# A convolution and whitening kernel: three x buffers instead of four, earlier read-back, one spin product a wait, and part of the packing on ScalarE

## The chip, the cores and the metric

The kernel runs on one core of a Trainium2 chip. The metric is the time of one execution in device microseconds; lower is better. Before the change, three runs gave 902.16, 902.56 and 902.67 us, so the median is 902.56 us. The engines are called as in the profile: PE (TensorE), DVE (VectorE), ACT (ScalarE), POOL (GpSimd) and SP (SyncE, which here only issues DMAs).

## The reference, cut to what matters

```python
# x: (4, 64, 256, 256) float32; L = 256, 64 channels, 4 images
def conv(x):                      # layer 0
    hx, hy = implicit_filter(...), implicit_filter(...)      # two small MLPs with sin, times a decay
    k = einsum('ijk,imk->ijmk', hx, hy)                      # per channel: an outer product of two 256-tap filters
    y = irfft2(rfft2(x, 512) * rfft2(k, 512))[..., :L, :L]   # a causal 2-D convolution, per channel
    return y + x * bias

def whiten(x):                    # layer 1
    x1 = x.transpose(1, 0, 2, 3).reshape(64, -1)
    x1_s = x1[:, ::9]                                        # every ninth pixel
    mean1 = x1_s.mean(-1)
    cov = x1_s @ x1_s.T / n + 0.01 * I
    W = isqrt_newton_schulz(cov, 5)                          # 64 x 64
    return (W @ (x1 - mean1)).reshape(...)
```

The filter of each channel is an outer product, so the 2-D convolution is two 1-D convolutions, and each of these is a product with a 256 x 256 Toeplitz matrix. No output pixel can be made before the covariance of all four images is known, because `W` depends on all of them.

## The kernel before, in words

**Two halves.** The first half makes the convolved images and writes them to a DRAM buffer `y_d`. The second half reads them back, multiplies by `W` and writes the output. Between them stands a short chain of small products, `whitening` (L460), that makes `W`.

**The first half.** A step is one channel group of 8 channels (`g`, 0 to 7) of one image (`n`, 0 to 3), so there are 32 steps, listed in `steps` (L107, L108). Groups 0 to 5 run one after the other, each over the four images; then the last two groups run image by image, so that image 0 is whole after step 25, and the others after steps 27, 29 and 31. A step has four chunks of two channels (`c` = 0, 2, 4, 6), and the text below calls chunk `c` of step `i` simply (i, c). For each chunk `group` (L394) issues the first Toeplitz products of this chunk together with the second Toeplitz products of the chunk two places earlier, 80 products in all. ACT then copies the first result out of PSUM (L409, four copies) and DVE adds bias times x to the second result and leaves it in the x tile (L412, two instructions). The eight PSUM banks hold two such groups. The very first and last chunks go through `half_group` (L266).

**What SP issues after each group.** SP's queue is in order. After each group come: `store` (L420), two DMAs of 256 KB from the x tile to `y_d` (L425); `load_x` (L100, issued at L588) of one chunk, 512 KB, of the step two ahead, into one of four x tiles; a block of the Toeplitz matrices of a later channel group, if the table `blocks` (L370 to L376) names this place; and, if the table `early` (L378) names it, the read-back of one piece of `y_d`, 2 MB, by `load_next` (L357).

**Packing.** For the covariance every ninth pixel has to be gathered from the x tile into the tile `samp[n]`. `pack_ops` (L313) makes nine instructions, one for each offset `s` (`copy_predicated` on DVE, L319). For groups 6 and 7 it is called for four channels at a time, for the others for eight. The instructions wait in a list `todo`, and after each group `pack(2.92)` (L385) hands out about 2.92 us of them by a cost that each carries. `covariance(n)` (L327) is 58 products over `samp[n]`; for image n - 1 it is put before chunk 2 of group 7 of image n. The last four channels of the last step are packed on PE (`pack_by_pe`).

**Read-back and homes.** A piece is 1/8 of an image, a tile of 128 x 4096 floats. It is read into a tile that the first half no longer needs. `homes` (L347) lists 13 such tiles in order: `e` (two tiles of `epool`), `t` (three Toeplitz tiles), `s` (four `samp` tiles) and `i` (four x tiles). Nine pieces are read by `early`, the other four behind the last step; 19 more follow as outputs leave.

**The chain.** `whitening` alternates one or two 64 x 64 products on PE with a small operation on DVE or ACT. In each wait `spin` (L437) puts products of the identity that nobody reads on PE: `spin(2)` six times in the loop of the chain (L522, L532, L540).

**The second half.** For each piece four rounds of products with `W` (L635); ACT adds the mean's share to one result (L639) and DVE to the other (L640), both writing back into the piece, and a DMA writes it out (L645). The piece's columns are held as two halves of 2048, and round `w` makes columns `w * 512` to `w * 512 + 511` of each half. Piece 0 leaves in four DMAs (two runs of 2 KB per partition each), piece 1 and the last two in two DMAs (two runs of 4 KB), all others in one (16 KB per partition). SP issues the DMAs of piece 0 and of the last 13 pieces, POOL the rest.

Of the kernel before, what the change touches and what calls it, by code (L numbers as in the profile page):

```python
# [38 lines left out]
F32 = mybir.dt.float32  # L39
I32 = mybir.dt.int32  # L40
AF = mybir.ActivationFunctionType
ALU = mybir.AluOpType
# [3 lines left out]
NB, C, L = 4, 64, 256  # L46
P, H2 = 128, 2
EMB, ORDER = 33, 64
PIX = L * L
CG = 8  # L50
HP = P // 2
STEP = 9
# [2 lines left out]
EPS = 0.01  # L55
N_ITER = 5
GW = P + L
FP = 4096

TURN = 6.283185  # L60
# [4 lines left out]
def conv_whiten_kernel(ctx: ExitStack, tc: tile.TileContext, a: dict, out: bass.AP):  # L65
    nc = tc.nc
    x = a["x"]

    const = ctx.enter_context(tc.tile_pool(name="const", bufs=1))
    xpool = ctx.enter_context(tc.tile_pool(name="xpool", bufs=4))  # L70
    epool = ctx.enter_context(tc.tile_pool(name="epool", bufs=2))
    spool = ctx.enter_context(tc.tile_pool(name="spool", bufs=NB))
    tpool = ctx.enter_context(tc.tile_pool(name="tpool", bufs=3))
    o1pool = ctx.enter_context(tc.tile_pool(name="o1pool", bufs=4))
# [25 lines left out]
    def load_x(t, g, n, c):  # L100
        nc.sync.dma_start(
            out=t[:, c : c + 2],
            in_=x[n, g][:, c : c + 2],
        )


    steps = [(g, n) for g in range(C // CG - 2) for n in range(NB)]  # L107
    steps += [(g, n) for n in range(NB) for g in range(C // CG - 2, C // CG)]  # L108

    x_tiles = [xpool.tile([P, CG, H2, L], F32, tag="in", name=f"x{u}") for u in range(4)]  # L110
    for c in range(0, CG, 2):
        load_x(x_tiles[0], *steps[0], c)
# [15 lines left out]


    rows = const.tile([P, STEP], F32, tag="rows", name="rows")  # L130
    pick = const.tile([P, STEP, P], F32, tag="pick", name="pick")

    def load_pick(lo, hi):
# [44 lines left out]
    nc.scalar.dma_start(out=g0_d[CG:], in_=taps[ORDER : ORDER + CG])  # L178
    nc.gpsimd.dma_start(out=g_d, in_=taps)
    nc.gpsimd.tensor_copy(rows, mask[:, NB - 1, 0, :])  # L180
    busy(22)

    def new_toeplitz(g):
# [129 lines left out]
    def pack_ops(g, n, yt, cs):  # L313
        def op(s):
            nj = (L - s + STEP - 1) // STEP
            src = yt[:, cs, :, s : s + STEP * (nj - 1) + 1 : STEP].rearrange("p c b j -> p b j c")
            dst = samp[n][:, :, 0:nj, g * CG + cs.start : g * CG + cs.stop]
            m = mask[:, n, :, s : s + 1].unsqueeze(3).to_broadcast([P, H2, nj, cs.stop - cs.start])
            nc.vector.copy_predicated(dst, m, src)  # L319

        cost = 0.3 + 1.5e-3 * H2 * NJ * (cs.stop - cs.start)
        return [(cost, lambda s=s: op(s)) for s in range(STEP)]

    cov = const.tile([P, C + 1], F32, tag="cov", name="cov")
    nc.gpsimd.memset(cov, 0.0)
# [1 line left out]
    def covariance(n):  # L327
# [18 lines left out]

    homes = [  # L347
        {"t": (tpool, "toep"), "s": (spool, "samp"), "i": (xpool, "in"), "e": (epool, "extra")}[k]
        for k in "eetssiistitis"
    ]  # L350

    def load_y(i):
# [16 lines left out]


    blocks = {}
    for g in range(1, C // CG):
        first = 16 * g - 14 if g < C // CG - 1 else 16 * g - 22
        for part in range(8):
            k = first + (part * 12 // 8 if g < C // CG - 2 else part)
            blocks[k // 4, k % 4 * 2] = (g, part)  # L376

    early = {  # L378
        (26, 4): 1, (27, 0): 1, (27, 4): 1, (28, 0): 1, (29, 2): 1, (30, 0): 1, (31, 0): 1, (31, 2): 1, (31, 4): 1
    }  # L380
    orders = [list(range(L // HP)), list(reversed(range(L // HP)))]

# [77 lines left out]
    def whitening(i15, ones):  # L460
# [57 lines left out]
        for k in range(1, N_ITER - 1):  # L518
            pq = product(T, T, f"pq{k}")
            if before is not None:  # L520
                next_z(k - 1, before)
            spin(2)  # L522
            Q = Qs[k % 2]
            nc.vector.tensor_copy(Q, pq)
# [25 lines left out]
        W = place(C)  # L550
# [6 lines left out]
    with tc.manual_schedule(  # L557
# [61 lines left out]
    for i, (n, q) in enumerate(pieces):  # L619
        yt = loaded.pop(i)  # L620

        v = yt.rearrange("p (v f) -> p v f", v=2)
        o = out[n, q].rearrange("p (v f) -> p v f", v=2)

        part = 512 if i == 0 else 1024 if i == 1 or i > len(pieces) - 3 else 2048
        for w in range(FP // 1024):


            cols = slice(w * 512, (w + 1) * 512)
            po = [  # L630
                psA.tile([P, 512], F32, tag="psA", name=f"po_{n}_{q}_{w}_{u}") for u in range(2)
            ]
            for k in range(2):
                for u in range(2):
                    nc.tensor.matmul(  # L635
                        po[u][halves[k]], lhsT=W[halves[u]], rhs=v[halves[u], k, cols],
                        start=True, stop=True,
                    )
            nc.scalar.activation(v[:, 0, cols], po[0], AF.Identity, bias=shift)  # L639
            nc.vector.tensor_scalar(v[:, 1, cols], po[1], shift, None, ALU.add)  # L640
            end = (w + 1) * 512
# [64 lines left out]
```

## Time and profile before

| what | value |
|---|---|
| median of three runs | 902.56 us |
| profiled execution, first to last instruction (its span) | 902.1 us, 0.4 us below the median |
| PE busy | 781.2 us, 87% |
| DVE busy | 581.5 us, 64% |
| ACT busy | 395.5 us, 44% |
| DMA | 285.61 MB |
| first product of the convolution | 16.49 us |
| last product of the convolution | 619.4 us |
| first product with `W` | 643.25 us |
| first output DMA issued | 645.57 us |
| last product with `W` done | about 847 us |

The shares are means over stages with different limits. Until 619 us PE is busy all the time; from 646 us on it is the DMA engines that are (PE is busy 82 of the 140 us from 700 to 840 us); between lie 24 us of packing, covariance and chain. A share of the whole span says little here: each part of the change has to be held against its own stage.

### The profile page before, as it was taken

The numbers are of one execution on the slowest core, as the hardware profiler recorded it, in microseconds if no ns is written. First come the engines' busy times: TensorE is split into PE (matmuls) and PEld (weight loads), VectorE is DVE, ScalarE is ACT, GpSimd is POOL, SyncE is SP. The second block draws the span as 40 slices with busy tenths as digits, with TensorE's granted clock in tenths as the row PEclk, the third lists the DMA queues.
The fourth block names the chain that finished last, engine by engine and source line by source line (L and its number), as shares of the span: only waits on it lengthen the run. The fifth ranks groups of instructions, "written<-read, shape, count | busy, mean of one in ns | idle before, by whom it ended". The sixth has DMA issues, their size and how long they took to land.

```text
span 902.1 us, 28046 instructions
## 1 busy us (share of the span) xinstructions
PE 781.2 (87%) x11928; PEld 647.5 (72%) x11928; DVE 581.5 (64%) x801; ACT 395.5 (44%) x676; POOL 14.5 (2%) x40
## 2 busy tenths in 40 slices
PE   8999999999999999999999999999999565666200
PEld 7999999999999999999999999999533111212000
DVE  3487778877888778877888877877688332233200
ACT  2655554545455555545454444442487232233200
POOL 1000000000000000000000000000010000000000
PEclk9999999999999999999999999999999766866755
DMA  7988889798788888888997899979999999999998
GB/s 209 327 262 252 242 261 271 234 273 251 247 263 261 244 264 259 258 250 267 293 275 241 285 351 356 335 237 390 375 401 429 430 432 432 429 434 430 430 430 355
DMA packets 117912, 285.61 MB, mean 317 GB/s; under 512 B 8891, under 2 KB 91116, under 8 KB 110108
## 3 DMA queue, kind: packets, MB, share of 16 engines
q1 hardware_dynamic: 113436, 244.94, 79.0%
q0 software_dynamic: 3056, 37.95, 10.0%
q8 instruction: 95, 1.56, 0.7%
q10 hardware_dynamic: 1296, 0.93, 0.4%
q14 instruction: 29, 0.24, 0.1%
HBM read 149.35 MB, written 134.44 MB: 315 GB/s over the span
## 4 chain that ended last, share of the span: by engine, by line
PE 74%; DMA 11%; another core or an unknown queue 7%; DVE 0%; issue 0%; SPq 0%; ACT 0%; POOLq 0%; DVEq 0%
PE p L220 64%; DMA out_dram<-yi 5%; DMA yi<-y_d 5%; PE po L635 4%; PE pc L333 2%; PE ph L252 1%; PE pk L300 1%; PE spin L442 1%; DMA toep<-g_d 0%; PE busy L152 0%; PE pm L158 0%; SPq L357 0%; DMA scratch<-in_zw_dram 0%; DVE yi L640 0%
## 5 line engine op out<-in xcount | busy, mean ns | idle before, releaser
L220 PE MATMUL p<-toep,x 64*64 64x64 f32 (+3 forms) x5040 | 579.5, 284 | 0.8 <-issue 0.8
L220 PE MATMUL p<-toep,o 64*64 64x64 f32 (+3 forms) x5040 | 579.5, 284 | 0.0
L220 PEld LDWEIGHTS p<-toep,x 64*128 64x128 f32 (+1 forms) x5040 | 535.7, 166 | 24.4 <-issue 1.3
L220 PEld LDWEIGHTS p<-toep,o 64*128 64x128 f32 (+1 forms) x5040 | 536.7, 166 | 10.7 <-issue 0.2
L409 ACT COPY o<-p 64x512 f32<-64x512 f32 x504 | 292.8, 581 | 294.2 <-PE p L220 286.6
L319 DVE COPY_PREDICATED samp<-mask,x 128x464 f32<-128x464 int32 (+3 forms) x351 | 297.2, 847 | 9.8 <-DVE x L412 0.2
L412 DVE SCALAR_TENSOR_TENSOR x<-x,bias,p 128x512 f32<-128x512 f32 x252 | 179.8, 744 | 121.3 <-PE p L220 117.3
L635 PE MATMUL po<-yi,chain 64*64 64x512 f32 x1024 | 143.7, 720 | 60.4 <-DMA yi<-y_d 60.4
L640 DVE TENSOR_SCALAR yi<-po,shift 128x512 f32<-128x512 f32 x128 | 96.1, 751 | 109.0 <-PE po L635 100.7
L635 PEld LDWEIGHTS po<-yi,chain 64*64 64x64 f32 x1024 | 48.0, 162 | 155.2 <-issue 150.5
L639 ACT ACTIVATE yi<-po,shift 128x512 f32<-128x512 f32 x128 | 88.0, 687 | 116.7 <-PE po L635 116.0
L333 PE MATMUL pc<-samp 128*64 128x65 f32 x464 | 14.9, 223 | 0.0
L333 PEld LDWEIGHTS pc<-samp 128*64 128x64 f32 x464 | 14.3, 137 | 0.3
L645 POOL DMA_DIRECT2D out_dram<-yi x19 | 10.5, 554 | 130.5 <-DMA out_dram<-yi 55.1
L606 POOL TENSOR_SCALAR chain<-ident 64x64 f32<-64x64 f32 x2 | 1.0, 519 | 606.6 <-PE ph L252 606.6
L286 DVE COPY o<-ph 64x256 f32<-64x256 f32 x8 | 3.4, 422 | 9.7 <-PE ph L252 9.6
L152 PE MATMUL busy<-idle 128*128 128x128 f32 x64 | 9.4, 307 | 0.0
L152 PEld LDWEIGHTS busy<-idle 128*128 128x128 f32 x64 | 8.9, 222 | 0.2 <-issue 0.2
L300 PE MATMUL pk<-x,pick 128*128 128x56 f32 (+1 forms) x72 | 8.3, 292 | 0.0
L300 PEld LDWEIGHTS pk<-x,pick 128*128 128x128 f32 x72 | 8.1, 192 | 0.1
L442 PE MATMUL spin<-ident 128*128 128x128 f32 x50 | 7.9, 292 | 0.0
L286 ACT COPY o<-ph 64x256 f32<-64x256 f32 x8 | 2.9, 368 | 10.7 <-DMA toep<-g_d 9.2
(93 smaller groups left out, 77.4 us busy)
## 6 DMA issues: line engine op xcount, KB each, us to landing
x<-in_x_dram SPq DMA_DIRECT2D x128, 512.0 KB, 5.3
y_d<-x SPq DMA_DIRECT2D x256, 256.0 KB, 3.5
yi<-y_d SPq DMA_DIRECT2D x32, 2048.0 KB, 15.6
out_dram<-yi POOLq DMA_DIRECT2D x17, 2048.0 KB, 67.7
out_dram<-yi SPq DMA_DIRECT2D x11, 2048.0 KB, 32.9
toep<-g_d SPq DMA_DIRECT2D x28, 256.0 KB, 6.3
toep<-g_d SPq DMA_DIRECT2D x29, 192.0 KB, 5.7
out_dram<-yi SPq DMA_DIRECT2D x4, 1024.0 KB, 32.8
```

The costliest lines, as they stand in the source:

```text
L152: nc.tensor.matmul(p, lhsT=idle[:, 0:P], rhs=idle[:, P : 2 * P], start=True, stop=True)
L220: mm = nc.tensor.matmul(ps[q : q + w, m, HP * k : L], lhsT=src[parts, k // 2, m * P + q : m * P + q + w], rhs=t[parts, : stop : -1] if k e ...
L300: nc.tensor.matmul(pk[:, b, :, 0:nj], lhsT=pick[:, (s - b) % STEP, :], rhs=yt[:, cs, b, s : s + STEP * (nj - 1) + 1 : STEP], start=(s == 0 ...
L319: nc.vector.copy_predicated(dst, m, src)
L333: nc.tensor.matmul(pc[half], lhsT=samp[n][:, b, j, 0:C], rhs=samp[n][:, b, j, :], start=(b == 0 and j < 2), stop=(b == H2 - 1 and j >= NJ ...
L409: nc.scalar.copy(o1[to], units[u][0][0][fr])
L412: nc.vector.scalar_tensor_tensor(x2[:, c2 + u], x2[:, c2 + u], bias[:, ch : ch + 1], units[u][1][0], ALU.mult, ALU.add,)
L442: nc.tensor.matmul(p, lhsT=ident, rhs=ident, start=True, stop=True)
L635: nc.tensor.matmul(po[u][halves[k]], lhsT=W[halves[u]], rhs=v[halves[u], k, cols], start=True, stop=True,)
L639: nc.scalar.activation(v[:, 0, cols], po[0], AF.Identity, bias=shift)
L640: nc.vector.tensor_scalar(v[:, 1, cols], po[1], shift, None, ALU.add)
L645: issue.dma_start(out=o[:, :, end - part : end], in_=v[:, :, end - part : end])
```

## The change

1. The x tiles are three instead of four, and `load_x` fetches the next step instead of the one after it. `x_of(i)` gives a step's tile. `epool` gets the tile that is freed, so there are still 13 homes, in the order `eeessstititis`.
2. `LATE = 3`: the last three channel groups instead of two run image by image, so images are whole after steps 22, 25, 28 and 31.
3. `blocks` is a table with new places and another order of the parts; `early` names (23, 4), (23, 6), (24, 0), (24, 4) and (27, 2) for one piece each, and (30, 2) and (31, 2) for two each. That is nine pieces, as before.
4. Of the packing of four channels, the instruction with `s == 0` becomes two ACT instructions (one for each `b`) that multiply by a new constant `base` (0 or 1) and so write all pixels; the other eight stay on DVE and write over it. `base` is made on POOL.
5. `spin(1)` instead of `spin(2)` at the three places in the loop of the chain.
6. A piece's columns are ordered so that round `w` makes 1024 adjacent ones; the output's layout and the host's transposition follow. The bytes per DMA stay, in one run per partition instead of two.

```diff
+LATE = 3
...
-    xpool = ctx.enter_context(tc.tile_pool(name="xpool", bufs=4))
-    epool = ctx.enter_context(tc.tile_pool(name="epool", bufs=2))
+    xpool = ctx.enter_context(tc.tile_pool(name="xpool", bufs=3))
+    epool = ctx.enter_context(tc.tile_pool(name="epool", bufs=3))
...
-    steps = [(g, n) for g in range(C // CG - 2) for n in range(NB)]
-    steps += [(g, n) for n in range(NB) for g in range(C // CG - 2, C // CG)]
+    steps = [(g, n) for g in range(C // CG - LATE) for n in range(NB)]
+    steps += [(g, n) for n in range(NB) for g in range(C // CG - LATE, C // CG)]
...
+    def x_of(i):
+        return x_tiles[(i + 1) % 3]
...
+    nc.gpsimd.tensor_copy(base, mask[:, :, :, 0])
...
-            nc.vector.copy_predicated(dst, m, src)
+            if s or cs.stop - cs.start == CG:
+                nc.vector.copy_predicated(dst, m, src)
+                return
+            for b in range(H2):
+                nc.scalar.activation(dst[:, b], src[:, b], AF.Copy, scale=base[:, n, b : b + 1])
 
         cost = 0.3 + 1.5e-3 * H2 * NJ * (cs.stop - cs.start)
-        return [(cost, lambda s=s: op(s)) for s in range(STEP)]
+        return [(cost if s or cs.stop - cs.start == CG else 0.0, lambda s=s: op(s)) for s in range(STEP)]
...
-        for k in "eetssiistitis"
+        for k in "eeessstititis"
...
-    for g in range(1, C // CG):
-        first = 16 * g - 14 if g < C // CG - 1 else 16 * g - 22
-        for part in range(8):
-            k = first + (part * 12 // 8 if g < C // CG - 2 else part)
-            blocks[k // 4, k % 4 * 2] = (g, part)
+    for g, (first, groups) in {
+        1: (2, 12), 2: (18, 12), 3: (34, 12), 4: (46, 12), 5: (57, 12), 6: (69, 12), 7: (82, 5)
+    }.items():
+        for at, part in enumerate((0, 2, 1, 3, 4, 6, 5, 7)):
+            k = first + at * groups // 8
+            blocks.setdefault((k // 4, k % 4 * 2), []).append((g, part))
 
     early = {
-        (26, 4): 1, (27, 0): 1, (27, 4): 1, (28, 0): 1, (29, 2): 1, (30, 0): 1, (31, 0): 1, (31, 2): 1, (31, 4): 1
+        (23, 4): 1, (23, 6): 1, (24, 0): 1, (24, 4): 1, (27, 2): 1, (30, 2): 2, (31, 2): 2
     }
...
-            spin(2)
+            spin(1)
             Q = Qs[k % 2]
...
-                spin(2)
+                spin(1)
                 T, M = Ts[k % 2], Ms[k % 2]
...
-                spin(2)
+                spin(1)
 
                 T = place(2 * C, rows=C)
...
-            load_x(x_tiles[1], *steps[1], c)
+            load_x(x_of(1), *steps[1], c)
         for i, (g, n) in enumerate(steps):
-            xt = x_tiles[i % 4]
+            xt = x_of(i)
...
-                if g == C // CG - 1 and n > 0 and c == 2:
+                if g == C // CG - 2 and n > 0 and c == 2:
                     covariance(n - 1)
...
-                if i + 2 < len(steps):
-                    load_x(x_tiles[(i + 2) % 4], *steps[i + 2], c)
-                if (i, c) in blocks:
-                    tg, part = blocks[i, c]
+                if 0 < i < len(steps) - 1:
+                    load_x(x_of(i + 1), *steps[i + 1], c)
+                for tg, part in blocks.get((i, c), ()):
...
-        v = yt.rearrange("p (v f) -> p v f", v=2)
-        o = out[n, q].rearrange("p (v f) -> p v f", v=2)
-
-        part = 512 if i == 0 else 1024 if i == 1 or i > len(pieces) - 3 else 2048
+        v = yt.rearrange("p (w v f) -> p w v f", v=2, f=512)
+
+        part = 1024 if i == 0 else 2048 if i == 1 or i > len(pieces) - 3 else 4096
...
-                issue.dma_start(out=o[:, :, end - part : end], in_=v[:, :, end - part : end])
+                issue.dma_start(out=out[n, q][:, end - part : end], in_=yt[:, end - part : end])
```

More of the change, by code (lines that the diff above doesn't have):

```diff
@@ L104, in load_x @@
         )
-    steps = [(g, n) for g in range(C // CG - 2) for n in range(NB)]
-    steps += [(g, n) for n in range(NB) for g in range(C // CG - 2, C // CG)]
-    x_tiles = [xpool.tile([P, CG, H2, L], F32, tag="in", name=f"x{u}") for u in range(4)]
+    steps = [(g, n) for g in range(C // CG - LATE) for n in range(NB)]
+    steps += [(g, n) for n in range(NB) for g in range(C // CG - LATE, C // CG)]
+    x_tiles = [xpool.tile([P, CG, H2, L], F32, tag="in", name=f"x{u}") for u in range(3)]
+    def x_of(i):
+        return x_tiles[(i + 1) % 3]
     for c in range(0, CG, 2):
-        load_x(x_tiles[0], *steps[0], c)
+        load_x(x_of(0), *steps[0], c)
         if c == 0:
@@ L130, in conv_whiten_kernel @@
     rows = const.tile([P, STEP], F32, tag="rows", name="rows")
+    base = const.tile([P, NB, H2], F32, tag="base", name="base")
     pick = const.tile([P, STEP, P], F32, tag="pick", name="pick")
@@ L620, in conv_whiten_kernel @@
         yt = loaded.pop(i)
-        v = yt.rearrange("p (v f) -> p v f", v=2)
-        o = out[n, q].rearrange("p (v f) -> p v f", v=2)
-        part = 512 if i == 0 else 1024 if i == 1 or i > len(pieces) - 3 else 2048
+        v = yt.rearrange("p (w v f) -> p w v f", v=2, f=512)
+        part = 1024 if i == 0 else 2048 if i == 1 or i > len(pieces) - 3 else 4096
         for w in range(FP // 1024):
-            cols = slice(w * 512, (w + 1) * 512)
             po = [
@@ L635, in conv_whiten_kernel @@
                     nc.tensor.matmul(
-                        po[u][halves[k]], lhsT=W[halves[u]], rhs=v[halves[u], k, cols],
+                        po[u][halves[k]], lhsT=W[halves[u]], rhs=v[halves[u], w, k],
                         start=True, stop=True,
                     )
-            nc.scalar.activation(v[:, 0, cols], po[0], AF.Identity, bias=shift)
-            nc.vector.tensor_scalar(v[:, 1, cols], po[1], shift, None, ALU.add)
-            end = (w + 1) * 512
+            nc.scalar.activation(v[:, w, 0], po[0], AF.Identity, bias=shift)
+            nc.vector.tensor_scalar(v[:, w, 1], po[1], shift, None, ALU.add)
+            end = (w + 1) * 1024
             if end % part == 0:
                 issue = nc.sync if i == 0 or i + len(homes) >= len(pieces) else nc.gpsimd
-                issue.dma_start(out=o[:, :, end - part : end], in_=v[:, :, end - part : end])
+                issue.dma_start(out=out[n, q][:, end - part : end], in_=yt[:, end - part : end])
         if i + len(homes) < len(pieces):
@@ L702 @@
     r = run_bass_kernel_spmd(nc, [arrays], core_ids=[0])
-    y = np.asarray(r.results[0]["out_0_dram"]).reshape(NB, PIX // H2 // FP, H2, C, H2, FP // 2)
-    return np.ascontiguousarray(y.transpose(0, 3, 4, 1, 2, 5)).reshape(NB, C, L, L)
+    y = np.asarray(r.results[0]["out_0_dram"]).reshape(NB, PIX // H2 // FP, H2, C, FP // 1024, H2, 512)
+    return np.ascontiguousarray(y.transpose(0, 3, 5, 1, 4, 2, 6)).reshape(NB, C, L, L)
```

## The prediction

> **What bounds the kernel now.** The page's busy table and slices come first, then the chain that ended last, stage by stage.
>
> ```profile
> PE 781.2 (87%) x11928; PEld 647.5 (72%) x11928; DVE 581.5 (64%) x801; ACT 395.5 (44%) x676; POOL 14.5 (2%) x40
> DMA  7988889798788888888997899979999999999998
> L220 PE MATMUL p<-toep,x 64*64 64x64 f32 (+3 forms) x5040 | 579.5, 284 | 0.8 <-issue 0.8
> ```
>
> The last row carries the first half: 126 groups take 579.5 us, so 4.6 us each, and PE idled 0.8 us before all of them. Nothing in the first half can make PE faster; an edit there can only make it wait. The chain then shows what lies between the halves:
>
> ```profile
> 636.41 0.29 PE pq L457 x2
> 636.71 0.64 PE spin L442 x4
> 637.35 0.26 PE pm L457 x2
> ...
> 643.25 27.70 PE po L635 x256
> ```
>
> PE goes from product to spin to product without a hole, so the unread products are on the path. The third stage is read from stretches of time (PE, PEld, DVE, ACT, POOL, clock, DMA share, GB/s):
>
> ```profile
> 508.00:520.00 12.00, 12.00 (x268) 11.34 (x268) 9.49 (x16) 4.66 (x8) 0.00 (x0) 1.00 1.01 358
> 534.00:546.00 12.00, 12.00 (x216) 11.29 (x217) 9.94 (x17) 4.96 (x9) 0.00 (x0) 1.00 1.03 393
> 570.00:580.00 10.00, 10.00 (x172) 9.46 (x170) 8.88 (x15) 5.37 (x10) 0.00 (x0) 1.00 1.00 380
> 646.00:662.00 16.00, 16.00 (x152) 5.66 (x148) 13.99 (x19) 12.88 (x19) 2.51 (x4) 1.00 0.97 345
> 664.00:700.00 36.00, 35.67 (x336) 12.55 (x329) 30.89 (x43) 28.33 (x42) 3.74 (x7) 1.00 1.01 431
> ```
>
> From 664 us the DMA engines are full at 431 GB/s. After the first output there are 32 pieces to write and 19 to read, 51 x 2.10 MB = 107 MB, or 248 us at that rate; the span has 256 us left. So the end is the moment `W` is known plus a fixed amount of traffic. The first three rows are stretches of the first half in which single pieces are read back: there, too, the DMA share is 1.0, at only 358 to 393 GB/s. These rows decide the prediction.
>
> **Part 1, the spins (faster).** Three turns of the loop, two waits each: six places lose one product of two passes, half of a spin's 0.64 us, so 0.32 us at most. PE then stands until its operand is there. In the timeline the first place reads:
>
> ```profile
> 636.64 0.71 PE L442 MATMUL spin<-ident 128*128 128x128 f32 x4
> 636.75 0.22 DVE L524 COPY chain<-pq 64x64 f32<-64x64 f32 x1 [0.31 <-PE pq L457]
> ...
> 637.28 0.33 PE L457 MATMUL pm<-chain 64*64 64x64 f32 x2
> ```
>
> One product ends at 636.96. The copy ends at 636.97, and PE starts 0.05 us (cov at L341 to pd) to 0.14 us (L503 to pq) after such an end, so `pm` starts at 637.02 to 637.11 instead of 637.28: 0.17 to 0.26 us. The same sum at the other five gives 0.24 to 0.32, 0.29 to 0.32, 0.17 to 0.26, 0.30 to 0.32 and 0.15 to 0.24. Together 1.3 to 1.7 us, I take 1.5. It reaches the end only if the DMA queue is empty by then. Before, the loads run out at about 645 us, when the rate drops to 201 GB/s for two microseconds; afterwards one piece fewer is asked for in the last two steps, so the queue is empty sooner. The clock is 1.00 through the chain, and PE would stand at most 0.15 us at a time. The Trainium skill (TensorE: Matmul & The Clock Gate, "Why this matters for your kernels") warns of PE gaps over about 3 us; no gap here comes near, so this rule would add nothing.
>
> **Part 2, one run per partition in the output DMAs (faster).** Only piece 0, piece 1 and the last two change; the others were contiguous. Stretches: 382 GB/s while piece 0 leaves in 2 KB runs (648 to 652 us), 412 in 4 KB runs (654 to 656), 431 in 16 KB runs, 416 at the end (890 to 898). Piece 0: 2.10 MB at 412 instead of 382 saves 0.4 us; piece 1 between 412 and 431, 0.2; the last two, 4.2 MB between 416 and 431, 0.2. Sum 0.8 us. Bounds: 0, and 3.8 if the whole shortfall of 646 to 662 us (16 x (1 - 345/431) = 3.2) and of the end (0.6) went; most of that is start-up, so I stay near the bottom.
>
> **Part 3, the first copy of four channels (nothing).** 15 packs of four channels give up one DVE instruction each:
>
> ```profile
> L319 DVE COPY_PREDICATED samp<-mask,x 128x232 f32<-128x232 int32 x60 | 37.6, 627 | 1.5
> L135 ACT ACTIVATE pick<-ident,rows 128x128 f32<-128x128 f32 x9 | 3.0, 394 | 0.1
> L309 ACT COPY samp<-pk 128x58 f32<-128x58 f32 x2 | 0.5, 226 | 12.1 <-DVE samp L319 10.8 <-PE pk L300 1.3
> ```
>
> DVE loses 15 x 0.63 = 9.4 us. ACT gains 30 instructions of 116 elements, between the rows of 58 (0.23) and 128 (0.39), so 0.36 each, 11 us; it waits 286.6 us for PE in this stage. There is a new wait: DVE's other eight write over what ACT wrote. Behind ACT's four copies (2.4 us after the group's end) and these two, DVE goes on at 3.1 us instead of 1.4. Queued behind it are the x instructions of the next group and, behind those on SP, the stores: up to 1.7 us late for a group. DVE's holes of 0.8 to 1.1 us a group and the 0.63 saved take that up; PSUM gives a whole group, 4.6 us, before PE notices. Without that cover it would cost up to 1.7 us for each of 15 packs. At the end DVE's packing is not late: its last write is at 625.9 us, PE's own packing ends at 627.6. `base`, one small POOL copy, comes before POOL has fences to pass.
>
> **Part 4, buffers and the table of read-backs (slower).** With four tiles an x chunk is asked for seven groups (32 us) before PE needs it, with three tiles three groups (13.8 us) before. SP's stores leave 1.4 us after the group's end. The three-buffer wait on the older tile's packing costs nothing: nine instructions at three a group are over before the load's turn. How long x loads take is in their view for 500 to 580 us:
>
> ```profile
> L101 SPq DMA_DIRECT2D x<-in_x_dram x15: 417/462/534, 502.4 to 575.1; - x15
> DMA to landing us min/median/max: 4.3/6.0/10.0
> ```
>
> 10 us happened behind one piece in the queue, and was covered. Afterwards four pieces come in four of five groups, and later two at once. Since all go through SP's queue, I count bytes. A group moves 0.52 MB of stores and 0.52 of x; a piece is 2.10. Count 1.4 us to the first issue, and 2.5 fixed (the shortest x landing in the trace, 3.9 us, less 1.3 of transfer).
>
> (25, 6), asked for after (24, 6): from (23, 4) on six groups' traffic and four pieces, 6.3 + 8.4 = 14.7 MB. Due when (25, 6) starts: eight groups and one covariance (3.64 us in the chain) later, 40.4 us. At 377 GB/s, the mean of the three rows by time, 38.9 + 3.9 = 42.8: PE waits 2.4 us.
>
> (31, 4), asked for after (30, 4): two groups and two pieces, 6.3 MB, due 4 x 4.6 = 18.4 us after (30, 2). 16.7 + 3.9 = 20.6: PE waits 2.2 us.
>
> (27, 2) has one piece, as (26, 4) had; no wait. The Toeplitz blocks add at most two parts of 0.25 MB a group, before step 22: no queue. Together 4.6 us. At 358 GB/s it is 7.6, at 393 2.4, and at 405 (the stretch from 612 to 640 us) 1.0 at (31, 4) alone. Nothing hides it: PE is the bound there, and all that follows waits for the last group. Image 0 being whole sooner gains nothing itself, as the number of homes, and so of reads left over, is the same.
>
> A rule against this change: the Trainium skill (DMA: Bandwidth & Descriptors, "Where 436 GB/s comes from") states that for transfers between HBM and SBUF the HBM side, about 358 GB/s a core, binds. The trace's 431 contradicts it; by the rule the waits would be 7.6 us and the time about 907.9.
>
> **Sum.** Span 902.1 - 1.5 - 0.8 + 4.6 = 904.4 us; the runs' median is 0.4 above the span: **904.8 us**.
>
> **Rivals.** *The queue keeps up.* If it drains near the 431 GB/s of the last stage while several pieces are queued, no x chunk is late, and the gains are left: 902.6 - 2.3 = 900.3 us, faster. It decides at 402 GB/s for (25, 6), 14.7 MB in 36.5 us, and at 434 for (31, 4), 6.3 MB in 14.5; between them up to 1.1 us of wait is left, 901.4. For it: a deep queue has fewer holes than the single reads of the three rows. Against: 405 in the deep queue after 612 us. 0.22 for a time over 0.2% faster, 900.76 and below.
>
> *One late chunk.* Near 393 to 405 GB/s only (31, 4) matters, 1 to 2.4 us in all, and gain and loss cancel: 901.3 to 902.7 us. With the upper end of no wait and the lower end of the forecast, the stretch within 0.2% (what a measurement of this kernel can tell from no change), 900.76 to 904.36, has 0.33.
>
> *The spins are not on the path.* If another operand is later than I read, the loop keeps its time: 906.3 us with the waits. Contained in the forecast's side, 0.05.
>
> *The forecast and worse*, 385 GB/s down to 358: 903.7 to 907.9 us; over 0.2% slower 0.45 in all.
>
> The likeliest is 904.8. The range takes in the queue that keeps up and the rate of 358: 900.0 to 908.0 us.
>
> **What would show it.** In the profile after: PE's idle time before L220, 0.8 us now, becomes 3 to 8 us, released by x loads, at (25, 2) to (25, 6) and (31, 4); six spins of two passes, and 1.3 to 1.7 us less from the first `pq` to `po`; about 400 GB/s in the first 10 us of output. No idle time at L220, or a gap elsewhere, would make the prediction wrong.

## The result, and the profile after

The changed kernel takes 910.92 us (median of four runs, 909.78 to 912.89); the kernel before took 902.59 us on the same chip. The ratio is 1.0095, with a 95% interval of 1.0081 to 1.0109. The direction was the forecast one, but the time lies above the range. The profiled run is the slowest of the four: it took 912.89 us and has a span of 911.1 us, 9.0 us more than the span before, where the medians differ by 8.3.

The page of the changed kernel (busy share of the span, granted PE clock and DMA in 40 slices, the convolution's products with their idle time) reads:

```profile
PE 783.3 (86%) x11916; PEld 647.7 (71%) x11916; DVE 570.8 (63%) x786; ACT 408.9 (45%) x706; POOL 14.0 (2%) x41
PEclk9999999999999999999999999999899878678855
DMA  7788788788888898898799786799799999999998
L227 PE MATMUL p<-toep,x 64*64 64x64 f32 (+3 forms) x5040 | 582.3, 285 | 4.5 <-issue 2.4
```

PE now idles 4.5 us ahead of its convolution products instead of 0.8, and the products themselves take 582.3 us instead of 579.5. Work that had not changed became slower. The chain that ended last (start, duration, what) shows where:

```profile
460.67 0.49 PE p L227 x18
461.16 2.40 issue
463.56 56.67 PE p L227 x934
...
594.32 13.81 DMA x<-in_x_dram
608.13 0.14 issue
608.26 11.16 PE p L227 x160
619.42 5.79 PE ph L259 x57
625.21 8.34 PE pk L307 x72
...
642.36 0.30 PE pq L469 x2
642.66 0.42 PE spin L454 x2
...
646.92 0.72 PE spin L454 x2
...
648.26 1.15 PE spin L454 x4
649.41 29.36 PE po L644 x256
```

There are two holes. The first, 2.40 us, lies inside a convolution group right behind the covariance of image 0; "issue" means that no semaphore held PE. The second, 2.06 us, is the wait for the x chunk of (31, 4), which landed 13.81 us after its issue. At the end the spins of two products last 0.42 us at first and then 0.72: the clock was halved while the chain ran. The stretches of time (PE, PEld, DVE, ACT, POOL, clock, DMA share, GB/s) show both clocks, and the start of the output:

```profile
594.00:608.20 14.20, 12.14 (x190) 10.70 (x186) 11.28 (x16) 8.25 (x15) 0.00 (x0) 1.00 1.01 393
608.20:612.00 3.80, 3.74 (x19) 3.77 (x21) 2.75 (x6) 0.91 (x2) 0.00 (x0) 0.55 1.15 379
646.00:648.00 2.00, 2.00 (x10) 1.43 (x9) 0.28 (x1) 0.21 (x1) 0.00 (x0) 0.50 0.94 401
655.00:658.00 3.00, 3.00 (x36) 1.00 (x32) 2.68 (x4) 2.48 (x4) 0.00 (x0) 1.00 1.01 404
658.00:660.00 2.00, 2.00 (x24) 0.64 (x20) 1.68 (x4) 1.50 (x3) 0.00 (x0) 1.00 0.33 125
660.00:662.00 2.00, 2.00 (x24) 0.71 (x20) 1.78 (x3) 1.66 (x3) 1.14 (x2) 1.00 0.74 242
```

Right behind the wait for (31, 4) PE runs at 0.55 of its clock; the group that follows takes 6.4 us instead of 4.6. Behind the first hole there is such a stretch too, 3.4 us at 0.50 from 465.0 us on. Between 658 and 662 us the DMA engines stand half empty, in the stage where they are the bound. POOL issues from the second piece on, and its timeline shows what is late: its first output comes 8.2 us after SP's first (652.33), while before it came 4.5 us after (650.03 after 645.57). The line below names ACT as what ended its wait, but that wait was over at 657.28 us, 3.3 us before the issue.

```profile
660.58 1.14 POOL L654 DMA_DIRECT2D out_dram<-yi  x2 [34.82 <-ACT yi L648]
```

So the 9.0 us of span are: 5.8 up to the end of the convolution (625.2 instead of 619.4), 0.2 from the first `pq` to the first `po` where 1.5 less was forecast, 0.6 from there to the first output, 2.2 in the output, and about level in between. The 5.8 hide a start-up that was 1.2 us shorter in this run (first product of the convolution at 15.27 instead of 16.49 us). From that product to the end of the convolution it is 7.0 us more: 3.6 of idle time and twice 1.7 for the two stretches at half clock.

### The profile page after: what moved, and what is told of

It reads as the page before. It is cut to its first block, busy times and chain, and to the rows that moved or that the text cites. A ratio compares the mean times of both kernels' runs of the same rounds, so it can differ in the third digit from the quotient of the medians.

```text
span 911.1 us, 28029 instructions
## 1 busy us (share of the span) xinstructions
PE 783.3 (86%) x11916; PEld 647.7 (71%) x11916; DVE 570.8 (63%) x786; ACT 408.9 (45%) x706; POOL 14.0 (2%) x41
## 4 chain that ended last, share of the span: by engine, by line
PE 72%; another core or an unknown queue 11%; DMA 9%; DVE 1%; issue 1%; SPq 1%; ACT 0%; POOLq 0%; DVEq 0%
PE p L227 62%; DMA out_dram<-yi 5%; PE po L644 4%; DMA yi<-y_d 2%; PE pc L344 2%; DMA x<-in_x_dram 2%; PE ph L259 1%; PE pk L307 1%; PE busy L158 1%; PE spin L454 1%; SPq L368 0%; PE pm L164 0%; DMA scratch<-in_zw_dram 0%; DVE yi L649 0%
## 5 line engine op out<-in xcount | busy, mean ns | idle before, releaser
L227 PE MATMUL p<-toep,x 64*64 64x64 f32 (+3 forms) x5040 | 582.3, 285 | 4.5 <-issue 2.4
L327 DVE COPY_PREDICATED samp<-mask,x 128x464 f32<-128x464 int32 (+3 forms) x336 | 287.7, 856 | 27.9 <-ACT samp L330 18.9
L330 ACT ACTIVATE samp<-x,base 128x116 f32<-128x116 f32 x30 | 13.7, 505 | 28.5 <-DVE samp L327 28.4
```

What stands on the lines that cost most here:

```text
L227: mm = nc.tensor.matmul(ps[q : q + w, m, HP * k : L], lhsT=src[parts, k // 2, m * P + q : m * P + q + w], rhs=t[parts, : stop : -1] if k e ...
L330: nc.scalar.activation(dst[:, b], src[:, b], AF.Copy, scale=base[:, n, b : b + 1])
```

## The experiments

Names that begin with a_ are the changed kernel with the edit shown, those with b_ the kernel before. Times are medians, ratios go to the kernel before on the same chip; what separates two runs is worked out as the difference of their ratios times 902.6 us. By the intervals of the ratios such a difference is uncertain by 0.8 to 1.7 us.

### First: are the waits for x due to the pieces in the queue?

**a_spread** puts the nine pieces further apart.

```diff
-        (23, 4): 1, (23, 6): 1, (24, 0): 1, (24, 4): 1, (27, 2): 1, (30, 2): 2, (31, 2): 2
+        (23, 4): 1, (24, 2): 1, (25, 0): 1, (26, 0): 1, (27, 2): 1, (30, 2): 1, (30, 6): 1, (31, 2): 2
```

> The changed kernel with its nine early read-backs spread out: one piece each after (23, 4), (24, 2), (25, 0), (26, 0), (27, 2), (30, 2) and (30, 6), two after (31, 2). Theory 'collisions' (x chunks late behind several pieces, and PE's clock halved for a window after each wait): no idle time at the L227 products, no half-clock stretch before 619 us, convolution done at about 619.4 us as before instead of 625.2, time about 905. Rival 'depth' (three x tiles, or DVE waiting for ACT, cost by themselves): still 2 us or more of PE idle time or longer groups, time 909 or more.

Measured: 917.4 us, 1.0165 (1.0152 to 1.0179): slower, not faster. The wait at (31, 4) was gone and the convolution ended at 619.1 us, as before the change, though a stall of 1.63 us without a semaphore was left behind the first covariance. But then PE waited 1.84 us ahead of `pk` for DVE's last x results, and the clock was halved for 17.1 us behind that. The table was the cause of the wait at (31, 4), and another loss stood behind it.

**a_spin2** is the changed kernel with `spin(2)` again in the loop of the chain, **b_spin1** the kernel before with `spin(1)`, **a_spread_spin2** is a_spread with `spin(2)`.

```diff
-            spin(1)
+            spin(2)
```

> The changed kernel with spin(2) again in the loop of the chain. Theory 'clock' (with one product a wait PE is too little used and its clock is halved inside the chain): clock 1.00 from the first pq to the first products with W, from pq to po 6.8 us, first output issued 2.3 us after the first po instead of 2.9; 0.5 to 2 us faster than the changed kernel. Rival 'spins are on the path and the halved clock has another cause' (the waits for x before): the half-clock stretch stays, and the time rises by 1 to 1.5 us.

> The kernel before with spin(1) at the three places and nothing else. Prediction's step: pq to po 1.3 to 1.7 us shorter than 6.8, time 901.1. Theory 'clock': a half-clock stretch in the chain, pq to po 6.5 us or more, the first output up to 0.6 us later after po, time 902.3 to 903.5. Because the clock's windows are fixed in time, single runs may differ.

> Both edits: read-backs spread out and spin(2). If 'collisions' and 'clock' are the whole cause: 902 to 903 us, level with the kernel before (output layout then worth up to 0.8 us). If something else of the change costs (output layout, packing on ACT, three tiles): 904 or more.

Measured: a_spin2 911.82 us, 1.0098 (1.0085 to 1.0111), not to be told from the changed kernel. Its waits were 1.34 us behind the first covariance, 1.56 at (25, 6) and 1.94 at (31, 4); only behind the second of them was the clock halved, for 3.4 us. b_spin1 gave 904.29 us, 1.0013 (1.0001 to 1.0026), in two clusters: four runs from 901.3 to 902.6 and eight from 903.8 to 906.3. Its profile is of a run of 901.27 us, at full clock, and there the way from `pq` to `po` is 5.6 us instead of 6.8. a_spread_spin2 gave 918.06 us, 1.0177 (1.0162 to 1.0192), with 1.85 us of wait ahead of `pk` and 17.1 us of half clock: the spins had nothing to do with that loss.

### Second: who makes PE wait ahead of `pk`?

**a_spread_dve** is a_spread_spin2 with all nine copies of the packing on DVE. **a_clear** has a third table besides (the last line below), in which no piece is in flight at the first covariance. **b_act** is the kernel before with ACT's first copy and `base` alone.

```diff
-            if s or cs.stop - cs.start == CG:
-                nc.vector.copy_predicated(dst, m, src)
-                return
-            for b in range(H2):
-                nc.scalar.activation(dst[:, b], src[:, b], AF.Copy, scale=base[:, n, b : b + 1])
+            nc.vector.copy_predicated(dst, m, src)
...
+        (24, 4): 1, (25, 2): 1, (25, 6): 1, (26, 2): 1, (27, 4): 1, (30, 4): 1, (30, 6): 1, (31, 2): 2
```

> As a_spread_spin2 (read-backs spread out, spin(2)), and all nine copies of four channels on DVE again. Theory 'ACT in DVE's way' (each pack of four channels makes ACT wait for DVE's earlier copies and DVE for ACT, so the last x results come late to PE's own packing, and the clock is halved for 17 us): the gap of 1.85 us before the pk products and the half-clock stretch behind it go, pk takes 8.3 us instead of 15.2, time 907 or less, 11 us better. Rival 'three tiles and the order of steps make DVE late': gap and half clock stay, 917.

> As a_spread_dve, but no read-back is in flight while a covariance runs: one piece each after (24, 4), (25, 2), (25, 6), (26, 2), (27, 4), (30, 4) and (30, 6), two after (31, 2). Theory 'code' (PE stands 1.3 to 2.4 us behind the first covariance because its own instructions, fetched by DMA, come late behind a piece): that gap falls below 0.5 us and no half-clock stretch follows, time 2 to 4 us below a_spread_dve. Rival 'the covariance or a PSUM bank makes the gap': it stays near 2 us.

> The kernel before with ACT making the first of nine copies of four channels, and nothing else. Prediction's step: no change, 902.6. Theory 'ACT in DVE's way': DVE waits about 19 us for ACT over 15 packs, x results late at the end of the first half, a gap before pk of up to 2 us with a half-clock stretch behind it, 905 to 914; and if POOL's one more instruction is what delays its first output DMA, the 8 us show here.

Measured: a_spread_dve 904.8 us, 1.002 (1.0011 to 1.0028); a_clear 901.3 us, 0.9985 (0.9976 to 0.9993); b_act 915.59 us, 1.0147 (1.0134 to 1.016), above the 914 that was expected at most. ACT's copies, which the prediction took at nothing, cost 13.3 us alone and 14.2 us in a_spread_spin2, `base` included. The chain of b_act:

```profile
618.98 0.05 issue
619.03 1.27 DVE x L291 x3
620.30 0.04 issue
620.35 15.57 PE pk L302 x72
635.92 1.83 PE spin L448 x8
637.75 5.22 PE pc L339 x92
```

The chain of before at the same place:

```profile
619.39 8.21 PE pk L300 x72
627.60 0.92 PE spin L442 x8
628.52 3.66 PE pc L333 x116
```

And in b_act what PE waited for ahead of `pk` (total us, times, longest) and two stretches of its time:

```profile
PE pk L302 <- DVE x L291: 1.2, 1, 1.2
620.00:636.00 16.00, 15.65 (x73) 15.56 (x74) 3.87 (x9) 0.37 (x3) 0.00 (x0) 0.52 0.98 384
636.00:641.00 5.00, 5.00 (x69) 4.78 (x70) 0.22 (x1) 0.18 (x1) 0.00 (x0) 0.50 0.76 287
```

A wait of 1.23 us is followed by a packing of 15.57 us where the chain before has 8.21, by spins of 1.83 where it has 0.92, and by a covariance of 5.22 where it has 3.66. Those three are 9.8 us longer: PE ran at 0.52 of its clock from 620 to 636 us and at 0.50 from 636 to 641. The wait itself is the small part. a_spread_dve still has a stall of 1.95 us behind the first covariance, without a half clock behind it, and another of 0.70 us. a_clear has neither and is 3.2 us faster. Its page has no idle time ahead of the convolution's products any more:

```profile
L225 PE MATMUL p<-toep,x 64*64 64x64 f32 (+3 forms) x5040 | 578.1, 284 | 0.0
```

a_clear keeps the three x tiles, the order of the steps, the table `blocks` and the new order of columns, and is no slower than the kernel before. So those parts cost nothing that can be measured here.

**b_act_notlast** leaves the pack behind the last step to DVE and gives ACT the other fourteen; **b_act_base** makes `base` on DVE instead of POOL.

```diff
-            if s or cs.stop - cs.start == CG:
+            if s or cs.stop - cs.start == CG or (g, n) == steps[-1]:
```

> b_act with the pack behind the last step left wholly to VectorE; the other fourteen four-channel packs have ScalarE's first copy. Theory (of the fifteen packs only the one at the end of the first half costs PE time, because PE waits there for VectorE's last conversions, and the half clock follows from that wait): no gap before the packing, packing in 8.3 us, 904 to 906 with GpSimd's late outputs alone. Rival (VectorE's lateness has built up over all of the packs): the gap before the packing stays within 0.5 us of b_act's 1.23 and the time near 915.

```diff
-    nc.gpsimd.tensor_copy(base, mask[:, :, :, 0])
+    nc.vector.tensor_copy(base, mask[:, :, :, 0])
```

> b_act with base copied by VectorE instead of GpSimd. Theory A (GpSimd's first outputs are 8 us late because its one instruction more moves a fetch of its instructions to the start of the output): GpSimd's first output 4 to 5 us after SyncE's again, 2 to 3 us less than b_act: 912.5 to 913.5. Theory B (the lateness comes from elsewhere, for example from the full queue at a shifted time): 8 us after SyncE's still, 915 to 916. The gap before the packing and the half clock behind it stay in both.

Measured: b_act_notlast 906.04 us, 1.0041 (1.0029 to 1.0053), `pk` without a wait in 8.23 us and no halved clock. So 9.6 of the 13.3 us hang on one pack of fifteen. DVE's timeline around 617 us shows it, first in b_act:

```profile
613.01 1.40 DVE L418 SCALAR_TENSOR_TENSOR x<-x,bias,p 128x512 f32<-128x512 f32 x2
615.91 3.24 DVE L322 COPY_PREDICATED samp<-mask,x 128x232 f32<-128x232 int32 x5 [1.51 <-ACT samp L325]
619.03 1.66 DVE L291 SCALAR_TENSOR_TENSOR x<-x,bias,ph 128x256 f32<-128x256 f32 x4
```

and then in b_act_notlast:

```profile
612.76 1.39 DVE L418 SCALAR_TENSOR_TENSOR x<-x,bias,p 128x512 f32<-128x512 f32 x2
614.18 3.25 DVE L322 COPY_PREDICATED samp<-mask,x 128x232 f32<-128x232 int32 x5
617.32 1.65 DVE L291 SCALAR_TENSOR_TENSOR x<-x,bias,ph 128x256 f32<-128x256 f32 x4
```

The same five copies stand ahead of the last x results in both. In b_act they begin 1.5 us later, because they may write only after ACT has, and everything behind them on DVE is later by as much.

b_act_base gave 913.62 us, 1.0102 (1.0073 to 1.0131): five runs from 911.9 to 915.2 and one of 905.0. GpSimd's first output came 4.8 us after SP's (660.74 after 655.97), where b_act has 8.2 (664.23 after 656.06) and b_act_notlast 8.4. So the late output belongs to one small instruction more on POOL near the start of the program, some 640 us earlier, and not to ACT's copies. By the medians it is worth 2.0 us, and from the first output to the end the two profiles take 257.4 us instead of 259.6. That would be the larger part of the 3.7 us that b_act_notlast still loses; the ranges of the two runs overlap, and the interval of b_act_base is too wide to say what is left of them.

### Third: the price of the table, and of the rest

**b_runs** is the kernel before with the new order of the output's columns. **a_noact** is the changed kernel without ACT's copies and `base`; **a_burst** is a_noact with `spin(2)`, and differs from a_clear in the table `early` alone.

```diff
-        part = 512 if i == 0 else 1024 if i == 1 or i > len(pieces) - 3 else 2048
+        part = 1024 if i == 0 else 2048 if i == 1 or i > len(pieces) - 3 else 4096
```

> The kernel before with the new order of the output's columns alone. Prediction's step: 0 to 3.8 us faster, taken 0.8. Theory 'late POOL' (the first DMA that POOL issues comes 8 us after SP's first instead of 4.5, with a hole in the output): if the layout causes it, the hole shows here and the time is 1 to 3 us above before; if another part does, 4.5 us, and 0.5 to 1 us faster.

> The changed kernel with all nine copies of a four-channel pack on VectorE again (and without base); the table of read-backs, the output order and the single unread products stay. Theory (ScalarE's copies cost the changed kernel only GpSimd's late first outputs, since the gap before the packing is hidden behind PE's own lateness of 2 us at (31, 4)): 910.9 less 2.2 to 2.7, so 908 to 909; GpSimd's first output 4 to 5 us after SyncE's instead of 8.2, the wait of about 2 us before (31, 4) stays. Rival (the read-backs cost nothing, all of the loss is ScalarE's copies): 901 to 902 and no gap at (31, 4).

> As a_noact, with two unread products a wait in the loop of the chain. Against a_clear it differs by the table of read-backs alone, so it prices that part. Theory (waits of 2 us at (31, 4), 0 to 1.6 at (25, 6), 1.3 to 2.4 behind the first covariance, each followed by 3.4 us at half clock that cost about 1.7): 6 to 9 us over a_clear's 901.3, so 907 to 910. The prediction's sum (waits alone, 4.6 us): 906. Rival (read-backs are free): 901 to 902. Against a_noact: the single product is worth 1 us either way at most.

Measured: b_runs 901.54 us, 0.999 (0.9981 to 0.9998), so 0.9 us gained. Its stretch from 646 to 662 us:

```profile
646.00:662.00 16.00, 16.00 (x156) 5.71 (x152) 14.01 (x19) 12.75 (x19) 2.73 (x5) 1.00 1.01 384
```

That was 345 GB/s before. The chains do not enter it at the same moment, so only the time is a measure. From the first output to the end of the span b_runs takes 256.3 us and the kernel before 256.6, so its profile does not show where the 0.9 us are gained.

a_noact gave 909.0 us, 1.0072 (1.0059 to 1.0084), POOL's first output 4.75 us after SP's: ACT's copies and `base` cost the changed kernel 2.1 us. PE came late to the end of the first half in both (the changed kernel has no wait ahead of `pk`), so DVE's lateness was hidden and the late output alone was left: from the first output to the end it is 258.8 us in the changed kernel and 256.5 in a_noact. a_burst gave 908.24 us, 1.0072 (1.006 to 1.0084). Against a_clear that is 7.9 us for the table, where the forecast had 4.6. Its profile has a stall of 2.23 us behind the first covariance, with 3.4 us of half clock, and a wait of 1.62 us at (31, 4), with none.

**a_early** is a_clear with the changed kernel's first five places, **a_late** with its last four, each against a_clear's table.

```diff
-        (24, 4): 1, (25, 2): 1, (25, 6): 1, (26, 2): 1, (27, 4): 1, (30, 4): 1, (30, 6): 1, (31, 2): 2
+        (23, 4): 1, (23, 6): 1, (24, 0): 1, (24, 4): 1, (27, 2): 1, (30, 4): 1, (30, 6): 1, (31, 2): 2
```

> a_clear with the changed kernel's first five entries of early ((23, 4), (23, 6), (24, 0), (24, 4), (27, 2)); the last four pieces stay as in a_clear ((30, 4), (30, 6), (31, 2) twice). Theory (the pieces in flight at the first covariance cost a stall of 1.3 to 2.4 us without a semaphore and 1.7 us of half clock; (25, 6) costs 0 to 1.6): 3 to 4.5 us over a_clear, 904.5 to 906, a stall between 462 and 467 us, none at 606 to 611. By the prediction's count of bytes: 2.4 us at (25, 6) alone, released by an x load, 903.7. Rival (the stall is there whatever is read): no difference to a_clear, 901.3.

```diff
-        (24, 4): 1, (25, 2): 1, (25, 6): 1, (26, 2): 1, (27, 4): 1, (30, 4): 1, (30, 6): 1, (31, 2): 2
+        (24, 4): 1, (25, 2): 1, (25, 6): 1, (26, 2): 1, (27, 4): 1, (30, 2): 2, (31, 2): 2
```

> a_clear with the changed kernel's last entries of early ((30, 2) twice, (31, 2) twice); the first five pieces stay as in a_clear. Theory (two pieces at once behind (30, 2) make the x chunk of (31, 4) late by 1.6 to 2.1 us, and the half clock behind it costs 1.7): 3.3 to 3.8 us over a_clear, 904.6 to 905.1, one wait at 603 to 608 us, released by an x load, and none before. By the prediction's count of bytes: 2.2 us, 903.5. Rival (only the whole sequence makes it late): no wait, 901.3.

Measured: a_early 904.75 us, 1.0018 (1.0009 to 1.0026); a_late 905.16 us, 1.0022 (1.0012 to 1.0031). That is 3.0 and 3.3 us over a_clear, together 6.3 of the 7.9; the rest is within the intervals. a_early's chain has the stall behind the first covariance and no wait for an x chunk:

```profile
461.12 0.49 PE p L225 x18
461.61 2.31 issue
463.92 56.68 PE p L225 x936
```

a_late has none there, and one at the chunk of (31, 4); its PE timeline reads

```profile
605.11 0.45 PE L225 MATMUL p<-toep,x 64*128 64x256 f32 x1 [2.67 <-DVE samp L324]
```

The profile names a DVE copy, which ended at 605.05 us. That product does not read `samp`. The x chunk landed at 604.97, 14.45 us after its issue, and PE began 0.14 us later, as it did behind the landings in the changed kernel (608.13, 608.26) and in a_noact (609.68, 609.81). A second stall, of 0.98 us, ended at 611.46. The expectation had neither this stall nor a clock that stayed whole: a_late's is 1.00 all through the first half, and the half clock expected behind the wait did not come.

**a_clear_spin1** is a_clear with `spin(1)`.

> a_clear with one unread product a wait. Theory (the chain is shorter by 1.2 us where the clock stays whole, and longer by 0.2 to 1 us where it is halved, and which of the two changes from run to run): two clusters, near 900 and near 902.5, median within 1.5 us of a_clear's 901.3. The prediction's term: 1.5 us less in every run, 899.8. Rival (the clock is halved in every run): 902 and over throughout.

Measured: 901.53 us, 0.9986 (0.9977 to 0.9995), no gain over a_clear, and a spread from 900.6 to 903.2 in place of 900.4 to 901.9 rather than two clusters. Its chain, in a run of 901.28 us:

```profile
634.00 0.42 PE spin L448 x2
...
637.88 0.42 PE spin L448 x2
638.72 1.15 PE spin L448 x4
639.87 28.76 PE po L638 x256
```

From the first `pq` to the first `po` it took 6.1 us instead of a_clear's 6.8. But the clock was halved for 3.4 us from 638.6 on. From `po` to the first output it took 3.0 us instead of 2.1, and the gain was given back.

## Why the prediction was wrong, by its own steps

Each part is priced by the pair of runs that differ in it, in us of time (plus is slower):

| part | forecast | measured | by |
|---|---|---|---|
| 1, the spins | -1.5 | 0 | a_clear_spin1 and a_clear; a_noact and a_burst |
| 2, output runs | -0.8 | -0.9 | b_runs |
| 3, ACT's copies and `base` | 0 | +2.1 here, +13.3 alone | the changed kernel and a_noact; b_act |
| 4, the table | +4.6 | +7.9 | a_burst and a_clear |

The forecast's sum was 2.3 us; the measured parts add up to 9.1, and the change took 8.6. Of the 6.8 us between the two sums part 4 makes 3.3, part 3 2.1 and part 1 1.5. Part 4 is the term that was mis-sized most; part 3 is the one whose mechanism was wrong.

**Part 3 is the step whose mechanism failed.** It rested on two sentences: "At the end DVE's packing is not late", and `base` "comes before POOL has fences to pass", so that it costs nothing. The first is wrong for the last step. The prediction had named the new wait and its queue, 1.7 us for a group, and let PSUM's spare group absorb it; but the products that pack read DVE's x results themselves, and there no spare group helps. The pick products start 1.2 us late, and b_act_notlast shows that this one place makes 9.6 us of the 13.3. The changed kernel paid less only because PE was late itself: a_spread removed that lateness, and the loss came out at `pk`. Each instruction on ACT took 0.505 us where 0.36 was estimated from rows of ACT (two neighbours in size), and ACT waited for DVE, a direction that the prediction did not see. The rows of the changed kernel (busy, mean ns, idle before):

```profile
L330 ACT ACTIVATE samp<-x,base 128x116 f32<-128x116 f32 x30 | 13.7, 505 | 28.5 <-DVE samp L327 28.4
L327 DVE COPY_PREDICATED samp<-mask,x 128x464 f32<-128x464 int32 (+3 forms) x336 | 287.7, 856 | 27.9 <-ACT samp L330 18.9
```

The second is wrong in the output: b_act_base moved that one instruction, and POOL's first output was back at 4.8 us after SP's. In the changed kernel the 2.1 us are this part of the loss.

**Part 4 had part of the mechanism, and mis-sized the sum.** The wait at (31, 4) was forecast at 2.2 us and was 2.06, and 1.62 to 2.67 in the other runs with these two pieces behind (30, 2). The wait at (25, 6), forecast at 2.4, was 1.56 in a_spin2 and none in the changed kernel and in a_early. The count of bytes for it went at 377 GB/s, and with several pieces queued the queue moved 393 (594 to 608 us) and 419 (465 to 472 us). What the sum lacked stands in two rows: a stall of 1.3 to 2.4 us behind the first covariance, which is not a wait for x at all, and the half clock behind a stall. The prediction's sign was 3 to 8 us of idle time at these products, released by x loads: 4.5 came, but only 2.06 of them were released by an x load, so that the sum of idle time fell into the forecast is luck.

**The half clock is the term that was put at nothing.** "No gap here comes near, so this rule would add nothing" was said of the chain's gaps of 0.15 us, and part 4's waits of 2.2 and 2.4 us got no term for the clock at all. By the Trainium skill (TensorE: Matmul & The Clock Gate, "Why this matters for your kernels"), which warns of gaps over about 3 us, they would not have got one either. Here the clock was halved behind 1.23 us (b_act), 2.06 and 2.40 us (the changed kernel), and the measurement decides. The page's Part 1 gives a window of about 3.4 us and half the clock; that agrees with the stretches here, 3.4, 6.8, 17.1 and 20.5 us at 0.50, which are one, two, five and six windows. A short stretch costs about 1.7 us in the convolution, so both holes of the changed kernel came to nearly twice their length. That is not so in every run: of the 14 stalls of more than 1 us ahead of convolution products in the profiles of the a_ kernels and the changed one, 8 had a half clock behind them.

**Part 1** was nearly right in the chain while the clock stayed whole: b_spin1's profile saves 1.2 us there, where 1.3 to 1.7 were forecast. But with one product a wait the clock was halved in or behind the chain in three of the five profiles: in the changed kernel (6.8 us from 645.9 on), in a_spread and in a_clear_spin1. With two it was whole in all of them. In five pairs of kernels that differ in the spins alone the ratios differ by no more than 0.13%, in either direction. "PE would stand at most 0.15 us at a time" was no reason for the clock to hold.

**Part 2** was right in its size, 0.9 us (0.2 to 1.7); that the output DMAs themselves became faster is not shown.

Of the rivals, the queue that keeps up and the one late chunk were wrong: both had no stall but those of x. The spins that bring nothing came true, though the chain did get shorter; in the profiles that show a loss it is the clock's, and not another operand's.

What stays open: which stalls halve the clock. Length does not decide it: 2.67 us in a_late left it whole, and 1.23 us in b_act did not. A window that runs on its own, as Part 1 of that page has it, is what the traces show: in each profile every change of the granted clock lies on one grid of 3.41 us, and the grid lies differently from run to run. What seems to count is how much of a stall falls into one window of that grid. In the changed kernel it was 1.97 and 2.06 us; a_late's 2.67 us fell into two windows, 0.94 and 1.73. Of the 14 stalls all seven with 1.83 us or more in one window were followed by half clock; of the seven with 1.79 or less one was, the 1.56 us at (25, 6) in a_spin2. Ahead of the packing 1.23 us were enough, and in a_clear_spin1's chain 0.01, so idle time is not the whole measure. No run moved a stall alone.

The stall behind the covariance is most likely PE's wait for its own instructions. A queue that the profile calls "instruction" carries packets of 16 KB all through the run. In the changed kernel one ran from 461.37 to 462.32 us, behind two early pieces asked for at 452.89 and 457.13 us, and PE went on at 463.56. All 19 stalls of more than 0.25 us between 20 and 640 us that the profiles put down to no semaphore end 1.2 to 1.5 us after the end of such a packet. So does a_late's second stall (packet until 610.10, PE at 611.46), which its profile puts down to a POOL instruction that had ended at 610.57. a_clear had such packets at 457.85 and 462.41 and no stall, and a_early against a_clear shows that the pieces in flight bring it. No run moved a packet alone.

The best version is a_clear: `spin(2)`, packing on DVE, no piece in flight at the first covariance, the new order of columns. At 0.9985 (0.9976 to 0.9993) it beats both kernels; part 2 alone gave 0.9 of its 1.4 us.

## What to carry to other kernels

Price a new wait at the place where its consumer has no spare buffer, not by the mean of the loop: of fifteen packs the last made 9.6 of 13.3 us. On PE, count a short stall up to twice, once for itself and once for the clock that may be halved behind it, and look at what follows: the dearest stalls here stood ahead of the packing products. Bulk reads put into an in-order queue cost most here where they met a short deadline or the place behind the first covariance, so move single pieces and read the gap of each.

## What the hardware showed that was not expected

- A wait of 1.23 us ahead of the packing products kept PE at half clock for 20.5 us in b_act, and of 1.84 us for 17.1 us in a_spread; behind the stalls ahead of convolution products it was 3.4 us, and once 6.8 (a_noact). Packing products of 128x56 do not bring the clock back as those of the convolution do; that the weight loads between them are the reason is argued, not shown.
- One more small instruction on POOL at the start of the program put its first output, some 640 us later, at 8.2 instead of 4.5 us behind SP's, and moving it to DVE put it back to 4.8 (b_act, b_act_base). In the changed kernel the semaphore wait ended at 657.28 us and the DMA was issued at 660.58, with 8 KB packets on a second "instruction" queue from 658.86 to 660.85. In all six profiled kernels with `base` on POOL the issue came 3.3 to 4.2 us after the end of the wait and 1.1 to 1.4 us after the end of such a packet; in the others it came 0.6 us after the end of the wait. A late fetch of POOL's instructions would fit that, and is not shown.
- ACT's instruction of 128x116 with a per-partition scale took 505 ns, more than the 394 ns of one of 128x128 in the profile before.
